# Pair 2's features around pair 0's propagation, pair 1's exponentials turned on TensorE, and column sums in column tiles

## The chip, the cores and the metric

The kernel runs on one core of one Trainium2 chip. The metric is the device time of one execution in microseconds (us), as the median of several runs. A core has TensorE (PE, matrix products), VectorE (DVE), ScalarE (ACT), GpSimd (POOL) and SyncE (SP), which here only issues DMAs; 16 DMA engines carry them out. All data are fp32.

## What is computed

There are 128 graphs of 128 nodes with 512 features, each with its own adjacency matrix `adj` of zeros and ones. Two layers follow each other, each ending in a residual and a layer norm:

```python
# layer 0: attention with 8 heads of 64 units
feats = einsum('bnf,hfu->bhnu', x, W)
dense = leaky_relu(e_self[..., :, None] + e_neigh[..., None, :], 0.2)
dense = dense + -1e10 * (1 - adj)
att = softmax(dense); out = relu(att @ feats + b)
x = layernorm(x + out)
# layer 1: hypergraph convolution, twice
#   conv(x, W, b) = Dn * H @ (Be * H^T @ (x @ W^T)) + b, with H = (adj != 0)
h = layer_norm(relu(conv(x, W1, b1)), gamma, beta)      # 1024 wide
x = layernorm(x + conv(h, W2, b2) + x)
```

`e_self` and `e_neigh` are the products of the features with two vectors for each head; Dn and Be are inverse degrees.

## The kernel before

The work goes in 64 pairs of graphs, and every tile holds both graphs of a pair (index g). Each pair passes these stages: x transposed (`x_transpose`, L382), features (`chain("pf", ...)`, L497, seven products and four `f_sum`), scores (`spread_rows` and `neighbours` by way of DRAM, then `masked` on POOL, `leaky` on ACT, `largest` on DVE, `exponential` on ACT), the exponentials turned (`e_write`, `e_read` and `e_transpose`, L621 to L643: written to DRAM in blocks of 32 columns, read back, and turned on DVE in blocks of 32), attention (`attend_pair`, L692), the first norm (`first_output`, L792), the propagation over the graph (`propagate`, tile pz, L814), the hidden layer (chain ph, h), the output layer (chain py, y2), the second propagation (pq) and the store.

The three big products are done by a scheme of Strassen's kind: the two graphs and the halves of a dimension make a 2 by 2 block product that is computed with seven products instead of eight. `chain` (L326) lists these seven (i = 1 to 7) with their times; the sums of weight blocks and of data blocks (xS, zS, hS) are made on POOL and DVE. Banks X, Y and W of PSUM collect the products; after products 1, 6 and 7 ACT copies bank X to SBUF (`copy`), and `f_sum`, `h_sum` and `y_sum` put the results together. `columns` (L93) issues a product as two matmuls of 64 stationary columns each, which stand in the two halves of the array.

The order of the work is written by hand. Each step has a lag (in pairs) and a time; the list `todo` holds (time, function) for all pairs, with T = 38.6 a pair, and is sorted by time at the end (L1232). Each engine executes its own instructions in that order, without reordering. The times are no measured times; only their order counts. The dictionary `first` (L1161) and two smaller ones give single steps of the first and last pairs other places. The start differs from the rest: pairs 0 and 1 compute plain features (`plain_features`, L516) from x turned on PE (`x_transpose_first`); pair 0's exponentials are turned on PE (`e_transpose_first`, L645, tile pet) and its attention is done in quarters (`attend`, tile pav). Also in the start the weights of the output layer are folded with gamma and beta: `prepare_output` (L272, tile pv) multiplies the 1024 rows of W2 with two columns (gamma/1024, beta) on PE, `prepare_output_sums` copies the two sums, and `prepare_output_spread` (L286) spreads each over all partitions by a product with a selecting matrix (tiles gw and bw); `prepare_output_blocks` (L295) applies gw to the four blocks of W2 on DVE.

DMAs of the start that matter: x, adj and weights in the order of lines 177 to 189; w2 on ACT's queue and w1 on both (L1140 to L1144); rd (`spread_rows`) and nb (`neighbours`) of pair 0 on SP and ACT; xb, the x of pair 2 in blocks (`load_blocks`, L122), on SP behind b2. A DMA signals one of eight semaphores in turn; the issue of the ninth waits until the first has landed, and so on.

Of the kernel before, what the change touches and what calls it, by code (L numbers as in the profile page):

```python
# [20 lines left out]
def kernel(  # L21
# [229 lines left out]
    gbs = const.tile([P, KH, 2], F32, name="gbs")  # L251
# [13 lines left out]
    def prepare_rows():  # L265

        made["sel"] = work.tile([2, 2, P], F32, tag="zT", name="sel")
        nc.gpsimd.tensor_copy(
            made["sel"], ident[:2, :2].unsqueeze(2).to_broadcast([2, 2, P])
        )  # L270

    def prepare_output():  # L272
        pv = made["pv"] = [bank(f"pv{j}") for j in range(2)]
        for blk, i, j in w2_blocks:
            for k in range(KH // 2):
                nc.tensor.matmul(
                    pv[j][:2, :QU], gbs[:, i * KH // 2 + k, :], blk[:, k, :],
                    start=(i == 0 and k == 0), stop=(i == 1 and k == KH // 2 - 1),
                )

    def prepare_output_sums():
        made["sums"] = const.tile([2, F], F32, name="sums")
        for j in range(2):
            nc.vector.tensor_copy(made["sums"][:, j * QU:(j + 1) * QU], made["pv"][j][:2, :QU])
# [41 lines left out]
    def chain(kind, lag, times, multiply, w, extra=0, since=0, until=PAIRS):  # L326
# [18 lines left out]

        for i, t in zip((1, 2, 6, 5, 7, 4, 3), times):
            at(lag, t, product, i, since=since, until=until)
# [190 lines left out]
    def spread_rows(p, s):  # L538
# [7 lines left out]
        shape = [B, NB, B] if p == 0 else [NB, B, B]  # L546
        rd = s["rd"] = dram.tile(shape, F32, tag="rd", name=f"rd_{p}")
        if p == 0:
            for b in range(NB):
                (nc.sync, nc.scalar)[b % 2].dma_start(rd[:, b, :], rows[b * B:(b + 1) * B])  # L550
        else:
            nc.sync.dma_start(rd.rearrange("b c j -> (b c) j"), rows)

    def blocked(p, t):

        dims = "p (h b j) -> p b h j" if p == 0 else "p (b h j) -> p b h j"
# [3 lines left out]
    def neighbours(p, s):  # L560
        s["nb"] = work.tile([P, 2, H * N], F32, tag="nb", name=f"nb_{p}")
        for g in range(2):
            dst, src, hs = s["nb"][:, g, :], s["rd"], slice((2 + g) * H, (3 + g) * H)
            if p == 0:
# [80 lines left out]
    def e_transpose_first(p, s, g, q):  # L645
        if (g, q) == (0, 0):
            s["eT"] = work.tile([P, 2, H, N], F32, tag="eT", name=f"eT_{p}")
        t = bank(f"pet_{g}{q}")
        for h in range(HH):
            n = (q * HH + h) * N  # L650
            nc.tensor.transpose(t[:, h * N:(h + 1) * N], s["nb"][:, g, n:n + N], ident)
        (nc.scalar.copy if q else nc.vector.tensor_copy)(
# [3 lines left out]
    for (g, q), tm, (lag, tl), (lagx, tx), te, tt in (  # L656
# [7 lines left out]
        at(2, tt, e_transpose, g, q, since=1)  # L664

    for g in range(2):
        at(2, (6.2, 10.9)[g], e_write, g, since=1)
        at(2, (10.0, 14.9)[g], e_read, g, since=1)
# [453 lines left out]
    for t, fn, *args in (  # L1122
# [24 lines left out]
        (120.7, prepare_hidden, (nc.gpsimd, 2)), (110.6, prepare_hidden, (nc.vector, 3)),  # L1147
# [128 lines left out]
```

## Time and profile before

| what | us |
|---|---|
| median of 3 runs (2398.81 to 2402.45) | 2401.5 |
| profiled execution, its own time | 2395.3 |
| its span (what the profile covers) | 2393.4 |
| PE / DVE / ACT / POOL busy in the span | 2360.8 / 2089.6 / 1528.5 / 1825.6 |
| one pair in the steady part, PE (pyY of one pair at 157.34, of the next at 193.90) | 36.6 |
| PE idle before its first matmul (waits for x) | 8.1 |

The profile is one execution. A row of the order in time has its start from the beginning of the span, the time from the first instruction's start to the last one's end, the engine, the line of the kernel, the operation, output tile and input tiles, the shape, and how many instructions follow each other; in brackets stands how long the engine was idle before and who released it. PE records each fp32 matmul of the program as two, and their ends are modelled, so lengths on PE are best read from one start to the next. A row of stretches has, for each engine, the busy time and the count of instructions, then the granted PE clock as a share of full speed, the busy share of the DMA engines and GB/s.

### The profile page before, as it was taken

To read this page: it belongs to the slowest core of one execution; us is meant where nothing else is said; L and a number is where in the kernel's file an instruction comes from. 1 tells how busy PE (TensorE), PEld (TensorE's weight loads), DVE (VectorE), ACT (ScalarE), POOL (GpSimd) and SP (SyncE) were. 2 spreads that over 40 slices of the span, in tenths; PEclk is the share of its full clock that TensorE was granted. 3 is DMA by queue.
4 is the path that set the end of the run, shared out by engine and by line. 5 is a ranking of instruction groups with operands and counts; after the bars stand their busy time and mean duration, and the time that the engine had idled before them with its cause. 6 is when DMAs were issued, how large, how long until landed. Compare 5 with 4: busy or idle time off the path is not lost.

```text
span 2393.4 us, 80729 instructions
## 1 busy us (share of the span) xinstructions
PE 2360.8 (99%) x32309; PEld 2026.8 (85%) x32309; DVE 2089.6 (87%) x4456; ACT 1528.5 (64%) x4481; POOL 1825.6 (76%) x2060
## 2 busy tenths in 40 slices
PE   7899999999999999999999999999999999999998
PEld 6788887888888888888888888888888888888886
DVE  7989888898898898898898888988988988988975
ACT  4565765756667667667667666666676676676662
POOL 5877786777877877877877778778778778778774
PEclk9999999999999999999999999999999999999999
DMA  6555454555554555555545555544545555555541
GB/s 197 133 148 150 143 144 134 159 143 147 151 148 144 149 148 148 151 143 154 144 142 157 141 147 155 146 146 147 150 143 153 147 150 139 148 156 140 149 128 37
DMA packets 431134, 347.09 MB, mean 145 GB/s; under 512 B 151440, under 2 KB 380328, under 8 KB 430760
## 3 DMA queue, kind: packets, MB, share of 16 engines
q1 hardware_dynamic: 427288, 337.46, 49.5%
q8 instruction: 256, 4.19, 0.7%
q10 hardware_dynamic: 3472, 4.47, 0.6%
q14 instruction: 118, 0.97, 0.2%
HBM read 239.08 MB, written 102.73 MB: 143 GB/s over the span
## 4 chain that ended last, share of the span: by engine, by line
PE 89%; DMA 4%; DVE 3%; ACT 1%; POOL 1%; issue 1%; SPq 1%; DVEq 0%; POOLq 0%; ACTq 0%
PE phX L97 17%; PE pyX L97 17%; PE pfX L97 8%; PE pyW L97 8%; PE phW L97 8%; PE pav L703 5%; PE phY L97 4%; PE pz L97 4%; PE pfW L97 4%; PE pq L97 4%; PE pyY L97 4%; PE pfY L97 2%; DMA ed<-nb 1%; PE pd L97 1%; DMA nb<-rd 1%
## 5 line engine op out<-in xcount | busy, mean ns | idle before, releaser
L344 ACT COPY py<-pyX 128x257 f32<-128x257 f32 x189 | 70.7, 374 | 538.5 <-PE pyX L97 465.6
L97 PEld LDWEIGHTS phX<-zS,w_sb 128*64 128x64 f32 x6144 | 350.6, 137 | 36.3 <-POOL ft L742 23.1
L97 PE MATMUL phX<-zS,w_sb 128*64 128x128 f32 x6144 | 373.4, 273 | 2.6 <-ACT ph L344 2.6
L904 POOL TENSOR_TENSOR sq<-sq 128x512 f32<-128x512 f32 (+2 forms) x384 | 343.9, 896 | 20.1
L589 POOL TENSOR_TENSOR nb<-nb,neg 128x512 f32<-128x512 f32 x256 | 319.9, 1284 | 23.1 <-DMA nb<-rd 12.7
L605 ACT ACTIVATE nb<-nb,ft 128x128 f32<-128x128 f32 x1020 | 325.1, 392 | 13.7 <-POOL nb L589 13.7
L619 ACT ACTIVATE nb<-nb,nm 128x128 f32<-128x128 f32 x1024 | 319.4, 392 | 4.2 <-DVE nm L611 4.0
L767 POOL TENSOR_TENSOR rso<-veo,mhalf 128x2 f32<-128x2 f32 x63 | 44.2, 701 | 338.4 <-DVE veo L765 338.4
L97 PE MATMUL pyX<-w_sb,hS 128*64 128x257 f32 x2016 | 245.1, 380 | 0.0
L97 PE MATMUL pyX<-w_sb,h 128*64 128x257 f32 x2016 | 243.7, 379 | 0.5 <-ACT py L344 0.5
L97 PE MATMUL pyW<-w_sb,hS 128*64 128x256 f32 x2016 | 243.3, 378 | 0.0
L881 ACT ACTIVATE h<-h,vecs 128x128 f32<-128x128 f32 x768 | 239.4, 394 | 2.0 <-DVE h L866 1.4
L611 DVE TENSOR_REDUCE nm<-nb 128x4 f32<-128x512 f32 x256 | 175.2, 684 | 48.8 <-ACT nb L605 46.2
L97 PEld LDWEIGHTS pyX<-w_sb,h 128*64 128x64 f32 x2016 | 173.7, 136 | 46.2 <-ACT py L344 0.9
L97 PEld LDWEIGHTS pyW<-w_sb,hS 128*64 128x64 f32 x2016 | 174.7, 136 | 43.6 <-issue 0.3
L742 POOL TENSOR_TENSOR ft<-ft,b_bc 128x512 f32<-128x512 f32 x128 | 203.9, 1613 | 6.1 <-ACT ft L533 6.1
L97 PEld LDWEIGHTS pyX<-w_sb,hS 128*64 128x64 f32 x2016 | 168.7, 137 | 38.7 <-issue 0.8
L640 DVE STREAM_TRANSPOSE eT<-eb 128x512 f32<-128x512 f32 x252 | 163.5, 685 | 5.7 <-DMA eb<-ed 4.7
L805 DVE SCALAR_TENSOR_TENSOR o<-y,b_bc 128x512 f32<-128x512 f32 x128 | 164.7, 1325 | 0.0
L1006 DVE SCALAR_TENSOR_TENSOR y<-y,rsh,bw_bc 128x512 f32<-128x512 f32 x126 | 150.1, 1229 | 14.9 <-POOL rsh L1002 14.9
L469 POOL TENSOR_TENSOR hS<-h 128x512 f32<-128x512 f32 x126 | 162.1, 1287 | 0.0
L892 ACT ACTIVATE sq<-h 128x512 f32<-128x512 f32 x256 | 160.6, 629 | 2.1
(178 smaller groups left out, 5672.4 us busy)
## 6 DMA issues: line engine op xcount, KB each, us to landing
nb<-rd SPq DMA_DIRECT2D x127, 512.0 KB, 5.6
ed<-nb SPq DMA_DIRECT2D x126, 512.0 KB, 3.4
eb<-ed SPq DMA_DIRECT2D x504, 128.0 KB, 2.9
x<-in_x_dram SPq DMA_DIRECT2D x64, 512.0 KB, 4.0
out_dram<-o SPq DMA_DIRECT2D x63, 512.0 KB, 2.9
xb<-in_x_dram SPq DMA_DIRECT2D x248, 128.0 KB, 5.5
a<-in_adj_dram SPq DMA_DIRECT2D x64, 128.0 KB, 2.4
w<-in_adj_dram SPq DMA_DIRECT2D x128, 64.0 KB, 5.0
```

Source lines behind the costliest of these rows:

```text
L97: nc.tensor.matmul(to[rows], lhs[:, rows], rhs, start=start, stop=stop, skip_group_check=True)
L469: engine.tensor_tensor(t[:, i], in0, in1, op=op)
L589: nc.gpsimd.tensor_tensor(t, t, neg[:, :, None, :].to_broadcast([P, NB, HH, B]), op=ALU.add)
L605: nc.scalar.activation(t, t, AF.Prelu, bias=s["ft"][:, g, h, 0:1], alpha=SLOPE)
L611: nc.vector.tensor_reduce(s["nm"][:, g, hs], scores(p, s, g, hs).rearrange("p b h j -> p h b j"), AX.XY, ALU.max, negate=True,)
L619: nc.scalar.activation(t, t, AF.Exp, bias=s["nm"][:, g, h:h + 1])
L640: nc.vector.transpose(s["eT"][:, g, hs, :].rearrange("p h (b i) -> p h b i", b=NB), s["eb", g][:, :, hs, :].rearrange("p b h j -> p h b j"),)
L742: nc.gpsimd.tensor_tensor(t, t, b0_bc.rearrange("p (h u) -> p h u", h=H), op=ALU.add)
L805: nc.vector.scalar_tensor_tensor(s["o"][:, g, :], s["y"][:, g, :], 2.0, b2_bc, op0=ALU.mult, op1=ALU.add)
L881: nc.scalar.activation(dst[:, k, :], src[:, k, :], AF.Relu, bias=b1_sb[:, c:c + 1])
L892: nc.scalar.activation(s["sq"][:, g, q * KH // 2:(q + 1) * KH // 2, :], hid(s, g, q), AF.Square, scale=DH ** -0.5,)
L904: nc.gpsimd.tensor_tensor(t[:, :n, :], t[:, :n, :], t[:, n:2 * n, :], op=ALU.add)
```

## The change

Only the start, the steps of the first four pairs and some places in the order change; the steps of a pair in the steady part stay.

- `prepare_output` computes the column sums in four column tiles of 32: the eight k blocks are shared out over four groups of 32 output partitions, with both column halves in one bank. `gbs` becomes 32 wide (filled with zeros, two columns used), and the spreading matrix `sel` now sums the four groups: it is made of `one`, a reduction of the identity.
- Pair 2: its four xb loads move from behind b2 to directly after pair 1's adj, its two x transposes on DVE ahead of pair 0's maxima, its x sums on POOL ahead of the first weight sums. Its features go on PE: products 1, 2, 6 and 5 after pair 0's attention, then gw, adj's transpose of pair 1 (pt) and product 7, then pair 0's pz, then products 4 and 3, then pair 0's hidden layer. Its rd and nb loads come earlier; its `edges` (and pair 3's loads of x and adj blocks) move too.
- Pair 1: `e_transpose_first` turns its exponentials on PE in four quarters between the products of pair 0's hidden layer; its scores are laid out by head as pair 0's are (rd written in four pieces), and `e_write`, `e_read`, `e_transpose` begin with pair 2.
- Around these, the gamma fold, the weight sums, bw, the skips, pair 1's `edges`, propagator and R, and some of pair 0's py steps get new places. In pair 0's py chain product 2 comes first after product 1 and pair 1's attention, so that product 7 follows product 6 directly.
- `product` and `copy` of a chain carry the chain's name, so that `first` can name them.

```diff
--- before.py
+++ after.py
@@ -248,7 +248,12 @@
         )[i]
         engine.tensor_tensor(dst, in0, in1, op=op)
 
-    gbs = const.tile([P, KH, 2], F32, name="gbs")
+    gbs = work.tile([P, KH, B], F32, tag="y", name="gbs")
+    nc.gpsimd.memset(gbs, 0.0)
+    one = small.tile([P, 2], F32, tag="one", name="one", bufs=1)
+    nc.vector.tensor_reduce(
+        one, ident.rearrange("p (c r) -> p r c", c=NB)[:, :2], AX.X, ALU.add
+    )
     made = {}
 
     def prepare_vectors():
@@ -264,24 +269,26 @@
 
     def prepare_rows():
 
-        made["sel"] = work.tile([2, 2, P], F32, tag="zT", name="sel")
-        nc.gpsimd.tensor_copy(
-            made["sel"], ident[:2, :2].unsqueeze(2).to_broadcast([2, 2, P])
-        )
+        made["sel"] = work.tile([P, 2, P], F32, tag="so", name="sel")
+        nc.gpsimd.tensor_copy(made["sel"], one.unsqueeze(2).to_broadcast([P, 2, P]))
 
     def prepare_output():
-        pv = made["pv"] = [bank(f"pv{j}") for j in range(2)]
-        for blk, i, j in w2_blocks:
-            for k in range(KH // 2):
-                nc.tensor.matmul(
-                    pv[j][:2, :QU], gbs[:, i * KH // 2 + k, :], blk[:, k, :],
-                    start=(i == 0 and k == 0), stop=(i == 1 and k == KH // 2 - 1),
-                )
+
+        t = made["pv"] = bank("pv")
+        for n in range(2):
+            for j in range(2):
+                for c in range(NB):
+                    k = 2 * c + n
+                    blk = w2_blocks[2 * (k // (KH // 2)) + j][0]
+                    nc.tensor.matmul(
+                        t[c * B:(c + 1) * B, j * QU:(j + 1) * QU], gbs[:, k, :],
+                        blk[:, k % (KH // 2), :], start=(n == 0 and j == 0), stop=(n == 1),
+                        skip_group_check=True,
+                    )
 
     def prepare_output_sums():
-        made["sums"] = const.tile([2, F], F32, name="sums")
-        for j in range(2):
-            nc.vector.tensor_copy(made["sums"][:, j * QU:(j + 1) * QU], made["pv"][j][:2, :QU])
+        made["sums"] = work.tile([P, F], F32, tag="sq", name="sums")
+        nc.vector.tensor_copy(made["sums"], made["pv"])
 
     def prepare_output_spread(c, name):
         made[name] = bank(name)
@@ -343,6 +350,7 @@
             t = s[kind, i] = work.tile([P, HALF if w == HALF else FW], F32, tag=f"{tag}_{i}", name=f"{kind}{i}_{p}")
             nc.scalar.copy(t[:, :n], s[kind, "X"][:, :n])
 
+        product.__name__, copy.__name__ = f"{kind}_product", f"{kind}_copy"
         for i, t in zip((1, 2, 6, 5, 7, 4, 3), times):
             at(lag, t, product, i, since=since, until=until)
         for i, t in enumerate(times[7:]):
@@ -543,17 +551,17 @@
             rows.rearrange("p (c x) -> p c x", c=2),
             s["ft"][:, :, :, :2].rearrange("p g h c -> p c (g h)"),
         )
-        shape = [B, NB, B] if p == 0 else [NB, B, B]
+        shape = [B, NB, B] if p < 2 else [NB, B, B]
         rd = s["rd"] = dram.tile(shape, F32, tag="rd", name=f"rd_{p}")
-        if p == 0:
+        if p < 2:
             for b in range(NB):
-                (nc.sync, nc.scalar)[b % 2].dma_start(rd[:, b, :], rows[b * B:(b + 1) * B])
+                (nc.sync, nc.scalar)[b % 2 if p == 0 else 0].dma_start(rd[:, b, :], rows[b * B:(b + 1) * B])
         else:
             nc.sync.dma_start(rd.rearrange("b c j -> (b c) j"), rows)
 
     def blocked(p, t):
 
-        dims = "p (h b j) -> p b h j" if p == 0 else "p (b h j) -> p b h j"
+        dims = "p (h b j) -> p b h j" if p < 2 else "p (b h j) -> p b h j"
         return t.rearrange(dims, b=NB, h=H)
 
     @step(1, 27.0)
@@ -561,7 +569,7 @@
         s["nb"] = work.tile([P, 2, H * N], F32, tag="nb", name=f"nb_{p}")
         for g in range(2):
             dst, src, hs = s["nb"][:, g, :], s["rd"], slice((2 + g) * H, (3 + g) * H)
-            if p == 0:
+            if p < 2:
                 src = src[hs].rearrange("h b j -> (h b j)")
             else:
                 dst = dst.rearrange("p (b x) -> p b x", b=NB)
@@ -645,11 +653,13 @@
     def e_transpose_first(p, s, g, q):
         if (g, q) == (0, 0):
             s["eT"] = work.tile([P, 2, H, N], F32, tag="eT", name=f"eT_{p}")
-        t = bank(f"pet_{g}{q}")
+        t = bank(f"pet_{p}_{g}{q}")
         for h in range(HH):
-            n = (q * HH + h) * N
-            nc.tensor.transpose(t[:, h * N:(h + 1) * N], s["nb"][:, g, n:n + N], ident)
-        (nc.scalar.copy if q else nc.vector.tensor_copy)(
+            nc.tensor.transpose(
+                t[:, h * N:(h + 1) * N],
+                s["nb"][:, g, (q * HH + h) * N:(q * HH + h + 1) * N], ident,
+            )
+        (nc.scalar.copy if q and p == 0 else nc.vector.tensor_copy)(
             s["eT"][:, g, q * HH:(q + 1) * HH, :].rearrange("p h n -> p (h n)"), t
         )
 
@@ -661,11 +671,11 @@
         at(lag, tl, leaky, g, q)
         at(lagx, tx, largest, g, q)
         at(2, te, exponential, g, q)
-        at(2, tt, e_transpose, g, q, since=1)
+        at(2, tt, e_transpose, g, q, since=2)
 
     for g in range(2):
-        at(2, (6.2, 10.9)[g], e_write, g, since=1)
-        at(2, (10.0, 14.9)[g], e_read, g, since=1)
+        at(2, (6.2, 10.9)[g], e_write, g, since=2)
+        at(2, (10.0, 14.9)[g], e_read, g, since=2)
 
 
 
@@ -1144,29 +1154,39 @@
         (15.46, load_weights, (nc.sync, w1_blocks[:1:-1], w1t, F // 2, HALF)),
         (16.1, everywhere, (b2_bc, b2, nc.sync)),
         (79.0, prepare_hidden, (nc.gpsimd, 0)), (79.1, prepare_hidden, (nc.gpsimd, 1)),
-        (120.7, prepare_hidden, (nc.gpsimd, 2)), (110.6, prepare_hidden, (nc.vector, 3)),
+        (120.7, prepare_hidden, (nc.gpsimd, 2)), (118.9, prepare_hidden, (nc.vector, 3)),
         (15.5, prepare_output_vectors, ()), (16.0, prepare_output, ()),
         (78.3, prepare_rows, ()), (78.79, prepare_output_sums, ()),
-        (78.99, prepare_output_spread, (0, "gw")), (98.0, prepare_output_spread, (1, "bw")),
-        (98.1, prepare_output_bias, ()), (98.2, prepare_output_blocks, (slice(0, 1),)),
-        (99.75, prepare_output_blocks, (slice(1, 2),)),
-        (117.8, prepare_output_blocks, (slice(2, 3),)),
-        (118.1, prepare_output_blocks, (slice(3, 4),)),
+        (78.995, prepare_output_spread, (0, "gw")), (123.2, prepare_output_spread, (1, "bw")),
+        (124.945, prepare_output_bias, ()), (112.0, prepare_output_blocks, (slice(0, 1),)),
+        (117.8, prepare_output_blocks, (slice(1, 2),)),
+        (119.0, prepare_output_blocks, (slice(2, 3),)),
+        (123.16, prepare_output_blocks, (slice(3, 4),)),
         (126.5, prepare_output_block_sums, (nc.gpsimd, slice(0, 2))),
-        (126.57, prepare_output_block_sums, (nc.vector, slice(2, 3))),
-        (141.0, prepare_output_block_sums, (nc.vector, slice(3, 4))),
+        (132.6, prepare_output_block_sums, (nc.vector, slice(2, 3))),
+        (144.2, prepare_output_block_sums, (nc.vector, slice(3, 4))),
         (100.0, prepare_mean_columns, ()),
     ]
 
     first = {
         ("spread_rows", 0): 13.5, ("neighbours", 0): 14.0,
         ("nodes", 0): 12.9, ("write_nodes", 0): 12.92, ("spread_nodes", 0): 15.9,
-        ("edges", 0): 14.46, ("edges", 2): 119.2,
-        ("x_transpose", 2, 0): 120.5, ("x_transpose", 2, 1): 121.1, ("scale_edges", 0): 14.47, ("propagator", 0): 14.55,
+        ("edges", 0): 14.46, ("edges", 2): 144.21, ("scale_edges", 2): 144.22,
+        ("x_transpose", 2, 0): 74.1, ("x_transpose", 2, 1): 74.2, ("x_transpose", 3, 0): 144.3,
+        ("x_sums", 2, 0): 78.71, ("x_sums", 2, 1): 78.72, ("x_sums", 2, 2): 78.73,
+        ("x_sums", 2, 3): 78.74,
+        ("pf_product", 2, 1): 78.991, ("pf_copy", 2, 0): 78.9915, ("pf_product", 2, 2): 78.992,
+        ("pf_product", 2, 6): 78.993, ("pf_copy", 2, 1): 78.9935, ("pf_product", 2, 5): 78.994,
+        ("pf_product", 2, 7): 78.997, ("f_sum", 2, 0, 0, 0, "Y"): 97.85, ("pf_copy", 2, 2): 110.35,
+        ("f_sum", 2, 1, 1, 2, "W"): 110.36, ("pf_product", 2, 4): 116.71,
+        ("pf_product", 2, 3): 116.72, ("f_sum", 2, 0, 1, 1, "W"): 116.8,
+        ("spread_rows", 2): 117.86, ("f_sum", 2, 1, 0, None, "X"): 117.85, ("neighbours", 2): 131.2, ("h_sum", 0, 1, 1, 2, "W"): 124.94, ("ph_copy", 0, 2): 124.93,
+        ("squares", 0, 1, 1): 144.15, ("squares", 0, 1, 2): 144.16,
+        ("skip", 0, 0): 126.58, ("skip", 0, 1): 132.5, ("py_product", 0, 2): 140.5, ("scale_edges", 0): 14.47, ("propagator", 0): 14.55,
         ("r_evict", 0): 97.845,
         ("spread_rows", 1): 15.72, ("nodes", 1): 15.55, ("write_nodes", 1): 15.85,
-        ("edges", 1): 110.4, ("scale_edges", 1): 110.5, ("neighbours", 1): 80.1,
-        ("propagator", 1): 121.7, ("spread_nodes", 1): 80.3, ("r_evict", 1): 121.8,
+        ("edges", 1): 97.95, ("scale_edges", 1): 97.96, ("neighbours", 1): 80.1,
+        ("propagator", 1): 130.3, ("spread_nodes", 1): 80.3, ("r_evict", 1): 144.23,
         ("leaky", 0, 1, 1): 77.65, ("leaky", 0, 0, 1): 73.6, ("largest", 0, 0, 1): 75.3,
         ("attend", 0, 0, 0): 78.95, ("attend", 0, 0, 1): 78.96, ("attend", 0, 1, 0): 78.97,
         ("attend", 0, 1, 1): 78.98, ("attended", 0, 0): 97.8, ("attended", 0, 1): 97.82,
@@ -1182,7 +1202,7 @@
         ("squares", 0, 0, 0): 141.3, ("squares", 0, 0, 1): 141.4, ("squares", 0, 0, 2): 141.5,
         ("nodes", 2): 149.8, ("write_nodes", 2): 149.9, ("spread_nodes", 2): 150.3,
         ("r_evict", 2): 160.4,
-        ("nodes", 3): 154.6, ("write_nodes", 3): 154.7, ("skip", 0): 132.5,
+        ("nodes", 3): 154.6, ("write_nodes", 3): 154.7,
     }
 
     def run(fn, p, args):
@@ -1194,16 +1214,18 @@
         (0, 12.6, plain_features, 1), (0, 12.65, adj_transpose_first),
         (0, 13.0, plain_features_out), (1, 13.1, x_transpose_out, 0), (1, 13.8, x_transpose_out, 1),
         (1, 14.5, plain_features, 0), (1, 14.6, plain_features, 1),
-        (1, 15.6, plain_features_out), (1, 97.9, adj_transpose_first),
+        (1, 15.6, plain_features_out), (1, 78.996, adj_transpose_first),
         (0, 78.8, e_transpose_first, 0, 0), (0, 78.85, e_transpose_first, 0, 1),
         (0, 78.9, e_transpose_first, 1, 0), (0, 78.93, e_transpose_first, 1, 1),
+        (1, 124.95, e_transpose_first, 0, 0), (1, 124.96, e_transpose_first, 0, 1),
+        (1, 130.41, e_transpose_first, 1, 0), (1, 130.42, e_transpose_first, 1, 1),
     ):
         todo.append((time, run, (fn, p, args)))
     for p in range(PAIRS):
         if p > 1:
-            todo.append(({2: 79.5, 3: 143.1}.get(p, p * T), load, (p,)))
-            todo.append((16.2 if p == 2 else p * T + (19.0 if p == 3 else 2.0), load_blocks, (p,)))
-            todo.append((p * T + (28.5 if p == 2 else 20.5), load_edges, (p,)))
+            todo.append(({2: 80.35, 3: 143.1}.get(p, p * T), load, (p,)))
+            todo.append(({2: 11.05, 3: 105.8}.get(p, p * T + 2.0), load_blocks, (p,)))
+            todo.append(({2: 105.7, 3: 146.85}.get(p, p * T + 20.5), load_edges, (p,)))
         for lag, time, name, pairs, fn, args in steps:
             if p not in pairs:
                 continue
@@ -1218,8 +1240,7 @@
                 }.get((name,) + args[:1], time)
             if p == LAST - 1:
                 time = {
-                    ("product", 2): 24.22 if (lag, time) > (3, 20.0) else time,
-                    ("product", 5): 29.5 if (lag, time) > (3, 20.0) else time,
+                    ("py_product", 2): 24.22, ("py_product", 5): 29.5,
                     ("squares", 0): 26.5, ("squares", 1): 26.6, ("h_sums", 2): 22.3,
                     ("h_rstd",): 4.6, ("y_scale", 1): 5.8, ("y_scale", 0): 5.9,
                 }.get((name,) + args[:1], time)
```

## The prediction

> **What bounds the kernel now.** First the page: the share of each engine.
>
> ```profile
> PE 2360.8 (99%) x32309; PEld 2026.8 (85%) x32309; DVE 2089.6 (87%) x4456; ACT 1528.5 (64%) x4481; POOL 1825.6 (76%) x2060
> ```
>
> TensorE (PE) is the bound of the whole. The change touches only how the first three pairs are threaded, so the second view is the busy time in stretches of 20 us (PE, PEld, DVE, ACT, POOL, then clock).
>
> ```profile
> 20.00:40.00 20.00, 19.18 (x138) 12.23 (x138) 15.18 (x42) 10.83 (x33) 12.33 (x11) 1.00 0.68 206
> 40.00:60.00 20.00, 15.95 (x230) 14.13 (x226) 19.45 (x51) 13.06 (x38) 11.83 (x15) 0.83 0.45 114
> 60.00:80.00 20.00, 18.05 (x240) 14.12 (x238) 19.72 (x27) 10.74 (x32) 18.63 (x14) 1.00 0.49 117
> 80.00:100.00 20.00, 17.16 (x244) 15.04 (x242) 19.16 (x47) 12.13 (x37) 16.37 (x23) 1.00 0.56 137
> 160.00:180.00 20.00, 20.00 (x292) 17.73 (x290) 15.52 (x33) 16.48 (x51) 16.68 (x20) 1.00 0.54 154
> ```
>
> From 160 on PE is full. From 40 to 100 it is not: there VectorE (DVE) is full, 19.45 to 19.72 of 20, with POOL at 18.63 beside it. What is won must be won before about 117 us, and on DVE rather than on PE. Third, PE in order of time (start, length, row, idle before it).
>
> ```profile
> 29.72 1.89 PE L276 MATMUL pv<-w_sb,gbs 128*2 128x256 f32 x8
> 36.73 1.97 PE L651 MATMUL pet<-ident,nb 128*128 128x128 f32 x16
> 47.23 3.68 PE L97 MATMUL pz<-R,y 128*64 128x128 f32 x32 [4.05 <-ACT y L794]
> 87.06 1.94 PE L97 MATMUL pz<-R,y 128*64 128x128 f32 x32
> 96.00 1.97 PE L97 MATMUL phX<-zS,w_sb 128*64 128x128 f32 x32 [1.92 <-ACT ph L344]
> 116.62 1.97 PE L703 MATMUL pav<-ft,eT 128*64 128x65 f32 x60 [1.72 <-DVE eT L640]
> ```
>
> The column sums pv fill PE from 29.72 to 36.73 (7.0 us); 4.05 us of idleness follow ahead of pair 0's propagation pz, which then runs at half pace (from 47.23 to the next row at 50.69, 3.46 us, against 1.75 at 87.06). Fourth, DVE and ACT in order of time around the same places.
>
> ```profile
> 32.87 4.77 ACT L619 ACTIVATE nb<-nb,nm 128x128 f32<-128x128 f32 x16
> ```
>
> ```profile
> 58.88 2.10 DVE L385 STREAM_TRANSPOSE xT<-xb 128x512 f32<-128x512 f32 x2
> ...
> 67.92 4.81 DVE L805 SCALAR_TENSOR_TENSOR o<-y,b_bc 128x512 f32<-128x512 f32 x2
> ...
> 84.75 0.41 DVE L935 TENSOR_TENSOR y<-py,pyW 128x256 f32<-128x256 f32 x1
> ```
>
> Pair 0's exponentials end at 37.64 and its PE transposes at 38.7. The y sum at 84.75 to 85.1 releases the last pyW of pair 0 and so pair 1's pz at 87.06. Last, the chain of waits: from 40 to 97 nearly all of its pieces are DVE's, then come a rsh on POOL, two round trips of ed and eb by DMA, and the eT that PE awaits at 116.62.
>
> **What the Trainium skill says.** "TensorE: Matmul & The Clock Gate", part 1: PE falls to half clock after about 3.4 us of idleness and needs as much activity to come back. The trace agrees (4.05 us idle, then 3.46 us for 1.75 us of work), and shows more: 2.32 us idle at 373.4 also left the following pav at 3.28 us to the next row instead of 1.77. "TensorEngine Tiling (Array Packing)", performance considerations: with at most 32 stationary columns, four column tiles, up to 4 times. The trace shows two tiles only: 8 pfX records of half width start to start in 0.89 us, against 1.89 for 8 full-width pf. "GPSIMD Engine Reference", specifications: GpSimd shares its SBUF interfaces with VectorE. Agrees: two hB (L435) took 0.48 us with POOL idle and 1.90 beside POOL; the two skips (L805) 1.82 at 101.07 and 4.81 at 67.92.
>
> **Part by part.** The sum is made against the profiled execution: 2395.3 us, of which 2393.4 is the span. The median of the runs shown is 6.2 us above it; I carry the difference over unchanged.
>
> *Column sums in tiles.* PE goes from 32 records of 0.219 us (7.0) to the same 32 in four columns: between 1.75 (full overlap) and 7.0 (none). I take 1.75. Yet the pets behind wait for exponentials that end at 37.64, so the only thing freed is the last pet's 0.5 us. Worth: 0 to -0.5, and PE gets a new hole of 1 to 2.5 us ahead of pet. The wider copy of sums (128x512, priced as the eT copy of 0.69, for two of 0.40) and the reduction "one" hide in DVE's idle time before 38; the memset and the wider sel hide in POOL's.
>
> *x blocks ahead.* Four loads (512 KB) join the first 20 us, where the DMA engines are 0.87 busy at 270 GB/s: 1.6 to 1.9 us of backlog. Behind it, by the rotation of DMA semaphores, stand SP's and ACT's rd writes and nb loads of pair 0, which waited in the old order for w2 loads as well. Bounds for nb: 0 to +1.5 us; I take +0.3, since the slice from 20 to 24 us moved only 36 GB/s. SP's later xb slot (2.96 us at 33.44) falls out, so pair 1's nb issue is no longer behind it.
>
> *Pair 2's transposes and x sums early.* Two of 1.05 us leave the full DVE stretch (58.88) and stand ahead of pair 0's maxima at 30.5. There the first maximum ends at about 33.3 instead of 31.3, and the exponentials start 0.5 later (32.87 to 33.4). That 0.5 cancels the 0.5 of pv. The four x sums (0.73 each) go into POOL's wait before 35.71. On the path: -2.1.
>
> *Pair 2's features around pz.* Five pieces (0.89 each), gw and pt stand between pav (ends 40.5) and pz: 40.5 + 4.45 + 0.9 + 0.44 = 46.3, before y is ready at 47.1. They are free and keep PE's clock up: pz takes 1.75, not 3.46, and the other two follow. The new waits: pt stands behind four of the pieces and ends at 45.4, and DVE's hT of pair 1 now waits for it at 45.6 (if PE is warm, nothing; if at half clock, 2 us or more, with all of DVE behind it). The f sum of W waits for ACT's third copy behind y: +0.5 on DVE. hB of pair 1 now meets POOL's masks: +1.0 (0 to 1.5, from 0.48 against 1.90).
>
> *Pair 1's exponentials on TensorE.* Two ed writes, eight eb reads go; 16 transposes (1.97 us) come on PE, 0.5 us in each of four gaps that it has; four DVE transposes of 0.65 become four copies of 0.69: nothing. No eT of pair 1 was late before (at 66.70 and 73.33 DVE did not wait), so the round trip saved is worth 0. Pair 2's nb is behind the last pet, about 66, still earlier than 78.54. SP is held there, and then by ab of pair 3 behind hT of pair 2 (77); hT of pair 3 needs it only near 88. The bw matmuls (0.9) move behind phW, where PE waits anyway.
>
> *Rest of the reordering.* The two skips part and the second meets an idle POOL (1.3 + 0.75 for 4.81: -2.7; bounds 0 and -3.4). The first-layer weight sum (L249) meets POOL's mask, +0.8, and DVE now waits for PE's ph chain in some four places between 58 and 66, about +1.6 together, which is what keeps the gain from growing. From 45.1 to the y sum: -2.1 + 0.5 + 1.0 + 0.8 - 2.7 + 1.6 = -0.9, and with the other meetings of the two engines (hB of pair 2, L226) at -1.1, about **-2.0**: y sum near 83.1, pz of pair 1 near 85. PE itself is then 3 us early and waits there, behind DVE. After it, POOL's masks of pair 2 start near 81 instead of 85.28, so that less of DVE's w and dn steps (86.14 to 90.5, 4.4 us for some 1.3) stands beside them: **-1.5** (0 to -3). Then nm, ed, eb and eT follow as a chain of fixed length: the pav of 116.62 moves to about 113.1. PE could go there earlier (4.6 us of holes from 87 to 117), but waits in the same places.
>
> Sum -3.5: 2391.8 profiled, **2398.0** as a median.
>
> **The rivals.**
> 1. *PE's holes close.* If DVE meets POOL less than I assume, or the chain behind pz loosens, the holes of 0.92, 1.92 and 1.72 us close on top: -3.5 - 4.6 = -8.1, 2393.4. For: PE has the work ready. Against: each hole ends with DVE, ACT or DMA, not with PE.
> 2. *Half clock: slower.* The hole ahead of pet and the sparse pets (0.12 us of work per 0.29 us exponential, from 33.8 to 38.3) throttle PE. pav takes 4 us, the first pieces 1.78 each, pt comes near 49.5, DVE stalls 3.8 us with everything behind it; then PE waits over 3 us for the y sum and is throttled a second time, pyW and pz at double length, +3.5. Ends of pz at 92.4 against 88.8; with 1.5 back later and 0.9 taken up by a hole, +3: 2404.5. It decides once DVE's stall at pt exceeds about 2 us and the second throttle comes too. For: 2.32 us sufficed once. Against: 1.92 us at 94 to 96 did not.
> 3. *Given back later.* From 227 to 310 the chain runs over rd, nb, ed and eb by DMA, and PE still lost 0.40 us at 314 and 2.32 plus 1.6 of clock at 375. If that loop and not the start sets the phase, PE arrives early and waits: no change, 2401.5.
> 4. *Tiles don't run side by side.* pv stays near 7 us; as it lies behind the exponentials, the time stays 2398.0. It is no case of its own, and lessens rival 2.
>
> **How the numbers follow.** Forecast 0.53 (own range 2395 to 2401, from the bounds of nb, hB and skips), rival 1 0.23, rival 2 0.12, rival 3 0.12. About 0.2% (4.8 us) is what a measurement can tell from no change: faster means below 2396.7. Faster: 0.21 of rival 1 and 0.15 of the forecast, 0.36. Slower, above 2406.3: part of rival 2 with a long throttle, 0.09. Same: 0.55. The range 2391.5 to 2404 leaves out the fast third of rival 1 and about half of rival 2.
>
> **What would show it.** Right: pv in about 2 us, yet pet's last record still ends near 38.5; pz of pair 0 at 1.75 us; the y sum of pair 0 near 83; DVE still over 19 of 20 from 40 to 80; pav of pair 2 near 113. Wrong: a clock below 0.9 from 30 to 50 with hT behind pt (rival 2), PE without holes from 87 to 117 (rival 1), or pav of pair 2 near 113 but a longer wait before 380 (rival 3).

## The result, and the profile after

| | before | after |
|---|---|---|
| median, us | 2401.97 (2398.81 to 2405.55, 4 runs) | 2420.62 (2417.09 to 2423.84, 4 runs) |
| profiled execution / its span | 2395.3 / 2393.4 | 2423.8 / 2422.0 |
| rows' store (rd) of pair 3 issued at | 117.2 | 118.0 |
| from there to the rd of pair 63 (60 periods) | 2189.5 | 2217.1 |

The change makes the kernel slower: 1.0077 times the time before, interval 1.0056 to 1.0098. The forecast of 2398.0 and its whole range are missed. The last two rows say where: of the 28.6 us between the spans of the two profiled executions, 0.9 arise in the start, which the change rewrites, and 27.6 in the 60 pairs after it, which it doesn't touch. These two executions lie further apart than the medians do, between which there are 18.7 us: 2395.3 is under all four runs of the kernel before, 2423.8 is the slowest of the four after. The issues of rd for pairs 3 and 63, before and then after:

```profile
117.15 0.34 SPq L552 DMA_DIRECT2D rd<-rows  x1
...
2306.65 0.34 SPq L552 DMA_DIRECT2D rd<-rows  x1
```

```profile
118.03 0.34 SPq L560 DMA_DIRECT2D rd<-rows  x1
...
2335.13 0.34 SPq L560 DMA_DIRECT2D rd<-rows  x1
```

From about pair 3 on the instructions of each engine are the same in both traces, one by one, and in the same order (on TensorE the last 31,668 matmul records, on VectorE the last 4,064 instructions, reads of its accumulator apart, on SyncE the last 1,837 transfers).

The page of the changed kernel: shares of busy time, one line of the DMA queues, and the shares of the chain that ended last.

```profile
PE 2366.5 (98%) x32325; PEld 2003.8 (83%) x32325; DVE 2080.4 (86%) x4456; ACT 1526.8 (63%) x4481; POOL 1822.2 (75%) x2061
...
q8 instruction: 256, 4.19, 0.7%
...
PE 69%; DMA 15%; POOL 5%; DVE 4%; ACT 3%; SPq 2%; issue 2%; DVEq 0%; ACTq 0%; POOLq 0%
```

TensorE had 89% of that chain before and DMA 4%. PE's waits after the change (who for whom, us in total, times, longest):

```profile
PE pav L713 <- DVE eT L648: 18.1, 15, 1.9
...
PE phX L97 <- ACT zT L839: 6.7, 11, 1.7
```

and before:

```profile
PE pav L703 <- DVE eT L640: 4.0, 2, 2.3
```

Attention (pav) now waits for its turned exponentials (eT) 15 times, up to 1.9 us at a time; the last such wait ends at 1169 us. The chain of one such period, in order of time (start, length, step; ed is the write of `e_write`, eb the read of `e_read`):

```profile
494.88 2.77 DMA rd<-rows
497.66 5.75 DMA nb<-rd
...
512.61 6.01 DMA ed<-nb
...
520.48 5.27 DMA ed<-nb
...
527.06 3.01 DMA eb<-ed
530.19 1.32 DVE eT L648 x2
531.64 1.97 PE pav L713 x60
```

Three transfers stand out: the rd store of 16 KB takes 2.77 us, the two writes of the exponentials 6.01 and 5.27. In a quiet period they take about 1.45, 3.2 and 3.5. So the question is what makes the same transfers late in one kernel and not in the other.

The start, for the rows that the prediction names (PE in order of time):

```profile
32.28 0.82 PE L283 MATMUL pv<-w_sb,gbs 128*32 128x256 f32 x10
...
35.72 4.89 PE L658 MATMUL pet<-ident,nb 128*128 128x128 f32 x16 [2.18 <-POOL sel L273]
...
50.51 1.97 PE L97 MATMUL pz<-R,y 128*64 128x128 f32 x32 [0.82 <-ACT y L804]
...
86.70 1.94 PE L97 MATMUL pz<-R,y 128*64 128x128 f32 x32
...
96.89 2.89 PE L97 MATMUL phX<-zS,w_sb 128*64 128x128 f32 x32 [2.41 <-ACT ph L351]
...
117.00 2.06 PE L713 MATMUL pav<-ft,eT 128*64 128x65 f32 x64
```

### The profile page after: what moved, and what is told of

Read it like the earlier page. It is cut to its first block, busy times and chain, and to the rows that moved or that the text cites. A ratio compares the mean times of both kernels' runs of the same rounds, so it can differ in the third digit from the quotient of the medians.

```text
span 2422.0 us, 80752 instructions
## 1 busy us (share of the span) xinstructions
PE 2366.5 (98%) x32325; PEld 2003.8 (83%) x32325; DVE 2080.4 (86%) x4456; ACT 1526.8 (63%) x4481; POOL 1822.2 (75%) x2061
## 4 chain that ended last, share of the span: by engine, by line
PE 69%; DMA 15%; POOL 5%; DVE 4%; ACT 3%; SPq 2%; issue 2%; DVEq 0%; ACTq 0%; POOLq 0%
PE pyX L97 13%; PE phX L97 13%; PE pyW L97 7%; DMA ed<-nb 7%; PE phW L97 6%; PE pfX L97 6%; PE pav L713 4%; PE pz L97 4%; PE phY L97 3%; PE pyY L97 3%; DMA nb<-rd 3%; PE pq L97 3%; PE pfW L97 3%; DMA rd<-rows 2%; DMA eb<-ed 2%; SPq L639 2%
## 5 line engine op out<-in xcount | busy, mean ns | idle before, releaser
L97 PEld LDWEIGHTS pyX<-w_sb,h 128*64 128x64 f32 x2016 | 168.4, 136 | 51.4 <-ACT py L351 0.9
```

The lines of the kernel that those rows point to most:

```text
L97: nc.tensor.matmul(to[rows], lhs[:, rows], rhs, start=start, stop=stop, skip_group_check=True)
```

## The experiments

Two theories stood against each other. **A, backlog:** the start leaves the transfer queue late, and each pair hands its backlog to the next. **B, fetch phase:** the q8 line above is TensorE's own instructions being fetched. It was on the page of the kernel before too, word for word. The trace has 256 such fetches of 16,384 bytes, four a pair, each taking about 1.05 us. A pair of the steady part has 252 matmuls, of which each leaves two loads and two products in the trace, and 14 semaphore instructions: 1022, two fewer than four fetches hold. The fetches therefore fall nearly on the same places of each pair and drift by 2 instructions (0.07 us) a pair.

The change gives TensorE 16 transposes more ahead of the steady part (pair 1's exponentials). A transpose, other than an fp32 product, leaves one load and one product. The records of pet, which are 32 loads and 32 products for the 32 transposes of pairs 0 and 1 (ns of one, first and last start):

```profile
L658 PEld LDWEIGHTS pet<-ident,nb x32: 137/143/183, 35.7 to 70.3; 128*128 128x128 f32 x32
L658 PE MATMUL pet<-ident,nb x32: 272/327/476, 35.7 to 70.4; 128*128 128x128 f32 x32
```

With three semaphore instructions more these are 35 instructions (the traces have 65,537 of TensorE before and 65,572 after), about an eighth of a fetch, and every later fetch comes some 1.2 us earlier within its pair (an estimate: 35 of 1022 instructions of a period of 36.37 us). The expectations below count a transpose as four instructions, which makes it 64 and 2.3 us; the phases that they name are therefore off by about 30 instructions, 1 us. That the lower count is right shows in the fetches themselves: by it the median fetch begins 204 instructions past the start of a block before and 209 after, while by four a transpose the two would lie some 30 further apart.

"Runtime: NRT & Kernel Launch", section "Instruction fetch mechanics", of the Trainium skill says that an engine's instructions are refilled in blocks of 16 KiB, 256 instructions, by a DMA queue of their own, and that crossing a block is "mostly hidden". The count agrees (65,572 instructions in 256 blocks); "hidden" holds for TensorE in the steady part (busy for 800.00 of 800 us in run 10 below, fetches and all), but not, it turns out, for the other transfers.

### 1 and 2: the phase alone, both ways

In the changed kernel (112 products) and in the kernel before (16), ahead of pair 0's first transposes; the products are overwritten and change no value:

```diff
         s["px"] = [bank(f"px_{p}_{g}") for g in range(2)]
+        for _ in range(112 if p == 0 else 0):
+            nc.tensor.matmul(s["px"][0][:B, :B], ident[:, :B], ident[:, :B], start=True, stop=True)
```

> The changed kernel with 112 tiny products (32x32) put on TensorE ahead of pair 0's first transposes, where it waits for x until 7.9 us. With the 16 transposes that the change adds they make 128, so that the 16 KB blocks in which TensorE's instructions are fetched fall on the same instructions of a pair as in the kernel before. Theory A (backlog: from pair 3 on both kernels run the same lists; the start only leaves the transfer queue late, and each pair hands its backlog to the next): the time stays at 2415 to 2426 us. Theory B (fetch phase: the 16 KB fetches now fall on the write of the exponentials and delay it): 2395 to 2406 us.

> The kernel before with 16 such tiny products in the same place, which moves its fetch blocks to where the changed kernel has them. Theory A (backlog): no change, 2398 to 2406 us. Theory B (fetch phase): 2414 to 2426 us, the loss without the change.

Measured: the changed kernel with 112 products 2398.71 (2394.13 to 2405.86), ratio to before 0.9997 (0.9985 to 1.0008). The kernel before with 16 products 2422.44 (2421.18 to 2425.56), ratio 1.0096 (1.0081 to 1.0111). The loss goes without undoing anything of the change, and comes without any of it. A is refuted, and B's times came. Neither run sets the phase of the other kernel exactly: with 112 products the fetches come some 30 instructions (1 us) later within a pair than in the kernel before, and with 16 they move by 63 instructions instead of the change's 35.

### 3 and 4: another order on SyncE

```diff
-    @step(4, 19.5, until=LAST)
+    @step(4, 19.5, since=LAST - 2, until=LAST)
     def store(p, s):
...
+    at(5, 7.0, store, until=LAST - 2)
...
-            todo.append(({2: 105.7, 3: 146.85}.get(p, p * T + 20.5), load_edges, (p,)))
+            todo.append(({2: 105.7, 3: 146.85}.get(p, p * T + 15.5), load_edges, (p,)))
```

> The changed kernel with SyncE's order of the steady part altered: the store of a pair's output stands behind the first write of the next pair's exponentials, and the four adjacency blocks ahead of the store of the degrees, so that nothing of theirs is queued just ahead of the rows' store. Theory A (backlog): the rows land about 1.4 us after their issue in nearly every pair instead of 3.2, the loop loses its carry, and the time falls to 2386 to 2398 us, under both kernels. Theory B (fetch phase): the write of the exponentials is as late as now, 2410 to 2424 us.

> The kernel before with the same order on SyncE. Theory A (backlog): its own loss between pairs 4 and 17 (about 7 us against a period of 36.37) goes, 2385 to 2397 us. Theory B (fetch phase): 2397 to 2405 us, no change.

Measured: 2466.0 (ratio 1.0274, 1.0252 to 1.0296) and 2451.48 (1.0215, 1.0198 to 1.0232): outside what either theory said, since the edit makes a wait of its own. In the kernel before with this order VectorE waits 60 times for the store that I had put later:

```profile
DVE o L805 <- DMA out_dram<-o: 121.2, 60, 5.4
```

The runs still tell something. The adjacency blocks are now issued some 5 us ahead of rd, with only the small store of the degrees between, and in pairs 4 to 13 rd nevertheless took 3.1 to 3.6 us, with a fetch 0.8 to 1.25 us after its issue. As the fetch drifts on, there is a sharp edge: in pairs 11, 12, 13, 15 and 16 rd takes 3.5 to 3.6 us with the fetch at 1.03 to 1.10 us; in pair 14 and from 17 to 26, with the fetch at 1.48 us or later, when rd has mostly landed, it takes 1.44 to 1.49 (once 2.22). That is a collision, not a queue.

### 5 to 7: the phase in steps

The edit of run 1, with 16, 32 and 48 products instead of 112.

> The changed kernel with 16 tiny products (32x32) on TensorE ahead of pair 0's first transposes. Theory B (fetch phase; a product is four instructions of 64 bytes, so 64 products fill one 16 KB fetch, and 16 move every fetch about 2.3 us ahead within a pair): the fetch that falls at 25 to 27 us of a pair now comes at 23 to 25, still in the flight of the second write of the exponentials: 2408 to 2432 us. Theory C (not the phase: products ahead of the start, whatever their number, warm or delay TensorE and so shift the start): 2394 to 2402 us, like the 112 products.

> The changed kernel with 32 tiny products there. Theory B: the fetches come at about 21, 15 and 34 us of a pair after the third; clear of the rows' store and of both writes at first, and on them later as the phase drifts by 2 instructions a pair (1022 against 1024): 2396 to 2414 us. Theory C: 2394 to 2402 us.

> The changed kernel with 48 tiny products there: with the 16 of the change they fill one fetch, and the phase is that of the kernel before. They lie wholly in TensorE's first wait for x, so the start isn't put back by about 2.8 us as it was with 112. Theory B: 2392 to 2398 us, faster than the kernel before. Theory C: between the time with 32 and that with 112.

Measured: 2434.4 (2431.94 to 2440.03), 2417.17 (2414.76 to 2419.14) and 2398.03 (2395.65 to 2402.27). With 0 products it is 2420.62, with 112 2398.71. The time doesn't follow how many products are added, but where they put the fetches: 16 make it worse, and 48 and 112, which differ by 64 products or one fetch, both take the loss away. Theory C, 2394 to 2402 us for 16 and for 32, falls. All three of my sizes were a little low (upper ends 2432, 2414 and 2398), and that 48 products beat the kernel before isn't shown (ratio 0.9995, 0.9987 to 1.0002). The 2.8 us that I expected to save with a shorter row didn't come: 32 or more products ahead of x delay the start all the same (rd of pair 3 at 120.5 with 32, 119.8 with 48, 120.9 with 112; 118.0 with none, 117.3 with 16); why, the runs don't show.

### 8 to 10: the phase held

Run 8 adds one tiny product in every second pair, to bring a pair to 1024 instructions on the mean; in its trace 30 semaphore instructions are gone with them, so it is 1023.5. Runs 9 (kernel before, 56 products ahead) and 10 (changed kernel, 40 ahead) reach 1024 by splitting a product that is there in every fourth pair:

```diff
+            w = N // 2 if g == k == 0 and p >= 4 and p % 4 == 0 else N
+            for c in range(0, N, w):
-            columns(
-                t[:, k * N:(k + 1) * N], s["y"][:, g, k * P:(k + 1) * P], s["R"][:, g, :],
+                columns(
+                    t[:, k * N + c:k * N + c + w], s["y"][:, g, k * P:(k + 1) * P],
+                    s["R"][:, g, c:c + w],
```

> The changed kernel with 40 tiny products ahead and one more in every second pair from pair 4 on, so that a pair holds 1024 instructions on the mean and the phase of the fetches doesn't drift; 30 more products of about 0.06 us. Theory B: no pair has a fetch in the flight of the rows or the exponentials, each period is 36.4 us, 2384 to 2392 us. Theory C: 2396 to 2402 us.

> The kernel before with 56 tiny products ahead (the fetches come about 1 us later within a pair) and, in every fourth pair from pair 4 on, one of the propagation's products split into two halves of 64 columns, so that a pair holds 1024 instructions on the mean and the fetches stay where they are. Theory B (fetch phase): no fetch in the flight of the rows' store or of the exponentials' writes in any pair; the 7.3 us that its steady part lies above 60 periods of 36.37 us go: 2386 to 2394 us. Rival D (the steady part has another cause of its stalls): 2397 to 2404 us.

> The changed kernel with 40 tiny products ahead and the same split instead of the 30 tiny products that cost 0.3 us each: the 9.6 us that they cost go. Theory B: 2388 to 2395 us. Against the kernel before with its phase held too it tells what the change itself does: my forecast's start (3.5 us earlier) would make it 3 us faster than that, a start that is late by the 0.4 to 1.2 us of the trace 0 to 2 us slower.

Measured: run 8 2400.93 (2398.6 to 2405.78), missed. Its fetches nearly stay (about 1.6, 16, 20.8 and 31.9 us after rd, from pair 4 to 62) and the stalls are gone, but every second period is 36.7 instead of 36.37: the odd product costs 0.3 us there, 30 of them 9, not the 0.06 that I took from a row of them. Run 9: 2392.62 (2390.52 to 2395.78), ratio 0.9965 (0.9951 to 0.9979). Run 10: 2391.48 (2389.62 to 2393.28), ratio 0.9961 (0.9949 to 0.9974). Both beat both kernels. Busy time in two stretches of 800 us, changed kernel first, then run 10 (PE, PEld, DVE, ACT, POOL, clock, DMA):

```profile
400.00:1200.00 800.00, 781.21 (x10764) 653.04 (x10762) 683.26 (x1474) 509.94 (x1503) 600.34 (x679) 1.00 0.52 144
1200.00:2000.00 800.00, 799.41 (x11082) 688.80 (x11079) 711.45 (x1515) 522.70 (x1538) 624.71 (x704) 1.00 0.53 148
```

```profile
400.00:1200.00 800.00, 800.00 (x11111) 685.31 (x11108) 710.49 (x1518) 524.26 (x1541) 624.33 (x704) 1.00 0.53 148
1200.00:2000.00 800.00, 799.49 (x11098) 682.87 (x11095) 708.47 (x1518) 523.29 (x1538) 623.11 (x705) 1.00 0.53 148
```

PE is full from 400 to 1200 in run 10, with the same instructions but for the split. SyncE's issues of one of its periods; a read is issued when the write ahead of it has landed, so the difference of starts is the landing time:

```profile
556.83 0.34 SPq L562 DMA_DIRECT2D rd<-rows  x1
558.32 1.78 SPq L580 DMA_DIRECT2D nb<-rd  x2
...
574.68 0.34 SPq L633 DMA_DIRECT2D ed<-nb  x1
578.37 1.85 SPq L641 DMA_DIRECT2D eb<-ed  x4
580.33 0.36 SPq L633 DMA_DIRECT2D ed<-nb  x1
584.12 1.73 SPq L641 DMA_DIRECT2D eb<-ed  x4
```

rd 1.49, ed 3.69 and 3.79, against 2.77, 6.01 and 5.27 above.

### 11: pair 2's x blocks where they were

```diff
-            todo.append(({2: 11.05, 3: 105.8}.get(p, p * T + 2.0), load_blocks, (p,)))
+            todo.append(({2: 16.2, 3: 105.8}.get(p, p * T + 2.0), load_blocks, (p,)))
```

> The same as the changed kernel with the held phase, but with pair 2's x blocks loaded where the kernel before loads them in SyncE's list (behind the weights' loads instead of ahead of them). If the early blocks hold up ScalarE's transfers and through them pair 1's features (1.9 us late at the first product of the degrees), the start comes 1.5 to 3 us earlier: 2386 to 2392 us. If the start is late for another reason: the same as with the early blocks within 1 us.

Measured on top of run 10: 2398.9 (2396.79 to 2401.06), 7.4 us slower than run 10, missed. Two rows of PE show both halves of it:

```profile
24.25 0.66 PE L97 MATMUL pd<-hT,hB 128*64 128x128 f32 x8
...
44.61 3.65 PE L660 MATMUL pet<-ident,nb 128*128 128x128 f32 x12 [14.08 <-POOL xS L479]
```

The early blocks do hold up ScalarE's transfers (with late blocks ScalarE issues nb of pair 0 at 23.68 instead of 27.22, and pd starts 4.6 us earlier than the 28.89 of run 10), but pair 2's x transposes and sums now stand ahead of pair 0's scores, and with late blocks pair 0 waits 14.08 us for them. The early load belongs to the early transposes.

### 12: the phase held in the bad place

The split of runs 9 and 10 in the changed kernel, with no product ahead.

> The changed kernel with the split only, and no tiny product: the fetches stay where the change puts them, on the rows' store and both writes. Theory B: the stalls of 1.2 us a pair no longer end near pair 31 but go on to the last: 2440 to 2475 us. Rival D (the stalls end for another reason, such as a backlog worked off): 2415 to 2426 us.

Measured: 2435.93 (2433.07 to 2442.72), ratio 1.0151 (1.0134 to 1.0168), 4 us below my lower end and far above rival D's. The stalls go on to the last pair (PE has 786.11 of 800 us before 1200 and 789.87 after):

```profile
PE pav L713 <- DVE eT L648: 28.0, 28, 2.3
```

So what ends them at about 1170 us in the changed kernel is the drift of the fetches: without it they don't end.

### What a fetch does to a transfer

The packets of the second write of the exponentials, changed kernel (issue at 520.48) and run 10 (580.33), from the DMA records of the trace; us after the issue:

```
                        changed        run 10
fetch of 16 KB          1.35 to 2.74   none
120 of 128 packets end  by 3.10        by 2.94
the last 8 end          3.69 to 4.80   2.94 to 3.32
landed                  5.28           3.79
```

A write of 128 partitions has 128 packets of 4 KB; eight are one sixteenth. They follow each other one by one, 0.16 us apart, and end 1.5 us later than the last of run 10, about the length of this fetch (1.39): it looks like one engine's share, held up while that engine fetched. Two sections of "DMA: Bandwidth & Descriptors" in the Trainium skill fit: "Queues, rings and completion order" says that one DMA engine serves several queues in turn, "Why a DMA increments its semaphore by 16 and not by 1" that a transfer has landed only when all its engines have signalled. That the eight are one engine's is inferred from their number; the records name no engine.

Over the twelve traces of runs 1, 2, 5 to 12 and of the two kernels, landing times (10%, median, 90%): rd with a fetch begun 0 to 1.0 us after its issue 2.62, 2.92, 3.20 (200 times), with none begun from 2 us before it to 4 us after 1.43, 1.47, 1.75 (80). The second ed with a fetch begun -0.2 to 2.3 us after its issue 4.48, 4.78, 5.39 (166), with none from 2 us before to 4 us after 3.29, 3.49, 3.78 (422). The bounds were read off these same traces. The first ed parts less well: its median is 4.98 with a fetch in that place (167) and 3.38 without (553), but a tenth of those without take over 6.12.

The page has a second row of fetches, q14, with 118 of them. They are 8 KB each and take about 0.42 us; the trace doesn't say which engines they serve. They do the same on a smaller scale: with no 16 KB fetch near, the second ed took 3.78 us with one of them begun -0.2 to 2.3 us after its issue and 3.48 with none (medians of 42 and 380).

A period without a stall is 36.37 us, and not the 36.6 given with the time before; the two rows of the kernel before are

```profile
157.34 1.94 PE L97 MATMUL pyY<-w_sb,h 128*64 128x257 f32 x16
...
193.71 1.94 PE L97 MATMUL pyY<-w_sb,h 128*64 128x257 f32 x16
```

By kernel: the products ahead, the shift of TensorE's instructions against the kernel before (counted in the traces, modulo the 256 of a fetch, the steady part's own additions left out), pairs of 60 in which rd or an ed was hit in this sense, and what the 60 periods took above 60 x 36.37 us. Hits and excess are of the one profiled execution, which can lie at either end of the runs; the median is of all runs.

```
                        products   shift   pairs hit   above, us   median, us
run 10 (held)           40         194     0           2.2         2391.5
run 11 (held)           40         194     0           1.8         2398.9 (late start)
run 9 (before, held)    56         223     1           5.3         2392.6
run 8 (nearly held)     40 + 30    194     1           10.1        2400.9
run 7                   48         226     12          9.6         2398.0
run 1                   112        226     14          6.9         2398.7
before                  0          0       16          7.3         2402.0
after                   0          35      28          34.9        2420.6
run 2 (before)          16         63      43          37.1        2422.4
run 6                   32         162     47          25.7        2417.2
run 5                   16         98      59          45.0        2434.4
run 12 (held)           0          35      60          50.2        2435.9
```

Without a held phase the time goes up and down with the shift, whichever of the two kernels it is: 2398 at 226, 2402 at 0, 2421 and 2422 at 35 and 63, 2434 at 98, 2417 at 162.

## Why the prediction was wrong, point by point

- **The rest after pav of pair 2, carried over unchanged: the step that failed.** The sum -3.5 ends at pav of pair 2, and the 60 pairs behind it got no term but rival 3. The instructions are unchanged indeed; the phase of their fetches is not. In the two profiled executions that cost 27.6 of the 28.6 us, and runs 1 and 2 take it away and bring it about by the phase alone.
- **Column sums in tiles:** right. The 32 records of pv take some 1.8 us from 31.60 (1.75 taken, 7.0 before), the four tiles run side by side, and a hole of 2.18 us opens ahead of pet (1 to 2.5 forecast). Worth nothing, as said.
- **"x blocks ahead", nb delay +0.3:** failed, by size and beyond its bounds of 0 to 1.5. ScalarE's issue of nb for pair 0:

```profile
20.36 1.72 ACTq L558 DMA_DIRECT2D rd<-rows  x2
...
25.52 0.35 ACTq L578 DMA_DIRECT2D nb<-rd  x1
```

  Before:

```profile
23.17 0.36 ACTq L570 DMA_DIRECT2D nb<-rd  x1
```

  That is +2.35 us. Run 11 shows the same hold (nb 3.5 us earlier without the early blocks). So pair 0's exponentials and pet end 2 us late (40.5 for 38.5 forecast).
- **Features around pz:** right in kind. pz at 50.51 takes 1.79 us to the next row at 52.30, no longer 3.46; all is late by the 2 to 3 us above (pt at 48.3 to 48.6 instead of 45.4).
- **VectorE's -2.0 at the y sum:** about right as a term. The sum of W ended at 84.8 (85.1 before, 83.1 forecast): the 2.35 us lost at nb are made up and 0.3 over, so the stretch itself gave some -2.7, by difference and if all of nb's delay reached it.
- **-1.5 behind it, pav of pair 2 near 113.1:** failed. pz of pair 1 starts 0.4 us earlier (86.70), but PE still waits 1.69 and 2.41 us behind it, and after the second wait two ph products run at 2.61 and 2.57 us for 1.75. pav is at 117.00, 0.4 later than before: from pz to pav 30.3 us instead of 29.6, where 1.5 less were forecast.
- **Pair 1's exponentials on TensorE, worth 0:** not tested as a saving; wrong in what it left out: its 32 instructions, with three semaphores, are what moved the fetches. This is the term put at nothing behind the step that failed.
- **Rival 1** didn't come: of the three holes 0.92 and 1.92 us grew to 1.69 and 2.41, and only the 1.72 ahead of pav closed. **Rival 2**: half its premise came (clock 0.82 from 20 to 40, pav of pair 0 3.1 us for 2.0 before), but VectorE was late anyway, and no second throttle followed at the y sum. Its +3 doesn't come out of its own terms either: 92.4 - 88.8 less 1.5 and 0.9 is 1.2. **Rival 3** named the right loop (rd, nb, ed, eb) and the wrong cause and price: PE wasn't early, the transfers were late.

No gain of the change itself is shown with the phase held in both: 2391.48 against 2392.62 side by side on one chip, five runs each, with intervals of their ratios to before that overlap nearly wholly (0.9949 to 0.9974 and 0.9951 to 0.9979). In their traces rd of pair 3 is issued at 119.65 and 119.72, so the start has won 0.1 us and not 3.5. Their phases aren't quite the same (shifts 194 and 223).

What stays open: why a phase at which nearly all pairs are hit costs 50 us in run 12 and 45 in run 5, why 47 pairs hit cost only 26 in run 6, and how far the first write's delay is the fetch's own and how far that of the loads queued ahead of it, which come late when rd does.

## What to carry to other kernels

When a loop's parts are unchanged and its time isn't, compare the landing times of the same transfers and read the instruction queue's line: a loop of nearly a whole number of fetch blocks keeps a collision for hundreds of microseconds. Before crediting or blaming an edit for a fraction of a percent, shift the instruction count by parts of a block (here 16, 32 and 48 products) and compare at the best phase. A loop padded to whole blocks, here by splitting a product rather than adding one, holds the phase that it has, a good one (2391.5) as well as a bad one (2435.9). And count the instructions in the trace: a product and a transpose don't leave the same number.

## What was unexpected of the hardware

- A 16 KB instruction fetch of about 1.05 us delays a 16 KB store by 1.4 us (medians 1.47 and 2.92) and a 512 KB write by 1.3 us (3.49 and 4.78), though such fetches are 0.7% of the DMA engines' time.
- 16 products of 32 columns that lie in an idle stretch of the start change the whole by 22 us (run 2, against the kernel before measured beside it), and 48 by -23 us (run 7, against the changed kernel).
- A single 32-column product between others costs a period 0.3 us (run 8: 36.70 for 36.37); in a row of 112 each takes 0.09 (from 1.79 to 11.95 us in run 1), in one of 48 0.11.
- An fp32 product leaves four instructions in TensorE's trace and an fp32 transpose two (pet: 16 loads and 16 products for 16 transposes).
